# A cross-attention and RWKV kernel on one core: probabilities turned by a second set of score products in place of transposes

## The chip, the cores and the metric

One core of one Trainium2 chip runs the whole program. The metric is device time in microseconds (us) from launch to end; the kernel was run three times, and the median counts. The profile is one further execution, seen by the hardware profiler. Engines are named as in the profile: PE multiplies matrices (PEld is its weight load), DVE, ACT and POOL work on vectors, SP issues transfers. SBUF is the memory on the core, PSUM the eight banks that PE writes, DRAM the memory beside the core.

## The reference, cut to what matters

Sixteen sequences of T = 112 tokens, width D = 512, attend with 16 heads of 32 to 375 context rows each; an RWKV block (token mixing, a recurrence along the tokens with decays, a gated feed-forward) follows. Everything is float32. The change lies in the attention:

```python
a = _layer_norm(audio_kv, ln_gamma, ln_beta)
Q = (hidden_states @ Wq.T).reshape(B, Tt, HEADS, HEAD_DIM).transpose(0, 2, 1, 3)
K = (a @ Wk.T).reshape(B, Ta, HEADS, HEAD_DIM).transpose(0, 2, 1, 3)
V = (a @ Wv.T).reshape(B, Ta, HEADS, HEAD_DIM).transpose(0, 2, 1, 3)
scores = jnp.einsum('bhtd,bhsd->bhts', Q, K) * scale
scores = jnp.where(mask, scores, jnp.float32(-jnp.inf))
attn = jax.nn.softmax(scores, axis=-1)
out = jnp.einsum('bhts,bhsd->bhtd', attn, V)
out = out.transpose(0, 2, 1, 3).reshape(B, Tt, D) @ Wo.T
return hidden_states + jnp.tanh(gate) * out
```

## The kernel before, in words

**Layout.** Activations lie with features on partitions: `x` is (128, 4 chunks, tokens), and a group g of two sequences (224 tokens) is worked at a time; there are eight groups. Four heads of 32 fill one chunk of 128 features, so a step of the attention is a pair (b, m): sequence b, chunk m, four heads. There are 64 steps.

**One step of the attention.** `scores` (L289) makes four products, one a head, with the query as weights (32 x 112) and the keys moving (375 columns). The four use the four row groups of PE, 32 rows each, and four PSUM banks of pool `ps_s`, which has four. The query is scaled by minus one over the root of 32, so the scores are negated and the softmax's maximum is a minimum here. L312 on DVE adds the mask, writes `pr` (112 tokens on partitions, 375 keys) and the row minimum `mn`. `exponentials` (L318) turns `pr` into exp(mn - pr) on ACT, with the row sums in `dens`. In the next step `transposed` (L328) transposes `pr` on PE in three thirds of 125 keys, four heads into one bank of `ps_s` for each third; L339 (ACT) or L341 (DVE) copies the bank to `prT` (125 keys on partitions, 4 x 112). For the first four sequences DVE copies two of three, after that one. In the step after that `outputs` (L344) multiplies by the values: 12 products, keys contracted, weights 125 x 32, into one bank of `ps_mm`, which has two; L356 copies it to `oR`. After four steps `divide` (L358) applies the sums.

**What runs beside it.** `context_units` makes keys (L237, copied by L243 to `kT`) and values (L248, L253) for the next sequence, `query_units` and `project_units` the projections through `project` (L175, matmuls on L181), whose weights come as slabs of 512 KB through SP (L154). The RWKV block has four parts for each group: `front`, `begin`, `middle`, `back`. `front` uses all four banks of `ps_s` three times a group (pxm, L588 and L603), and DVE takes them out in `mixed` (L565). `middle` is the recurrence, 16 steps n a group: `spread` (L744) loads the value rows of a step in four transfers kv<-vd from DRAM (L752, SP), two steps ahead; POOL and DVE multiply by the keys (L765); DVE scans (L788) with decays in PSUM and products in SBUF; POOL multiplies by the receptances (L792); PE sums (L804).

**What sets the order.** All parts are Python generators. A loop at the end of the kernel (L961) always advances the part whose place on a common scale is lowest; the amounts that a part yields are its costs, so the yields set how the parts interleave. The framework then orders each engine's instructions statically, by priority and readiness; `tc.high_priority(AHEAD)` puts an instruction 400 places ahead. It also sets all semaphores and gives out the buffers (`bufs` for each tag). `planned_after` adds an order without a wait. Every engine queue, SP's too, works in order: an instruction that waits holds those behind it.

Of the kernel before, what the change touches and what calls it, by code (L numbers as in the profile page):

```python
# [7 lines left out]
F32 = mybir.dt.float32  # L8
# [5 lines left out]
P = 128  # L14
# [35 lines left out]
def xattn_rwkv_kernel(ctx: ExitStack, tc: tile.TileContext, ins: dict, out: bass.AP):  # L50
# [39 lines left out]
    eps = keep.tile([P, 1], F32, name="eps")  # L90
    tgate = keep.tile([P, 1], F32, name="tgate")
    minus_half = keep.tile([P, NSC], F32, name="minus_half")
    wk = keep.tile([P, NC, D], F32, name="wk")
    wv = keep.tile([P, NC, D], F32, name="wv")
    maa1 = keep.tile([P, NC, NF * DM], F32, name="maa1")
# [14 lines left out]
    def load_mask(b, after=None):  # L110
        mrows[b] = sm.tile([T, S], U8, tag="mrow", name=f"mrow_{b}", bufs=2)
        load = nc.sync.dma_start(
            mrows[b], ins["mask_row"][b * S : (b + 1) * S].partition_broadcast(T)
        )
        if after is not None:
            planned_after(load, after)
# [97 lines left out]
    def context_units(b):  # L214

        raw = raws.pop(b)
        aT = ctxp.tile([P, NC, S], F32, tag="aT", name=f"aT_{b}")

        def turn(k):
            pt = mm_tile(f"pa_{b}_{k}")  # L220
            for c in range(NSC):
                nc.tensor.transpose(
                    pt[:, c * SC : (c + 1) * SC], raw[:, c, k * P : (k + 1) * P],
                    ident[:SC, :SC],
                )
            with tc.high_priority(AHEAD):
                nc.scalar.activation(
                    aT[:, k, :], pt[:, :S], AF.Identity, bias=vec(R_B0, k), scale=vec(R_G0, k)
                )

        kTs[b] = kT = []
        vs[b] = v = kvp.tile([SC, NSC, D], F32, tag="v", name=f"v_{b}")

        def key(m):
            pk = mm_tile(f"pk_{b}_{m}")
            for k in range(NC):
                nc.tensor.matmul(  # L237
                    pk[:, :S], wk[:, k, m * P : (m + 1) * P], aT[:, k, :],
                    start=(k == 0), stop=(k == NC - 1),
                )  # L240
            kT.append(kvp.tile([P, S], F32, tag="kT", name=f"kT_{b}_{m}", bufs=6))
            with tc.high_priority(AHEAD):
                nc.scalar.copy(kT[m], pk[:, :S])  # L243

        def value(c):
            pv = mm_tile(f"pv_{b}_{c}")
            for k in range(NC):
                nc.tensor.matmul(  # L248
                    pv[:SC, :], aT[:, k, c * SC : (c + 1) * SC], wv[:, k, :],
                    start=(k == 0), stop=(k == NC - 1),  # L250
                )
            with tc.high_priority(AHEAD):
                nc.scalar.copy(v[:, c, :], pv[:SC, :])  # L253

        return (
            [(0.5, lambda k=k: turn(k)) for k in range(NC)]
            + [(2.6, lambda m=m: key(m)) for m in range(NC)]
            + [(3.5, lambda c=c: value(c)) for c in range(NSC)]
        )
# [29 lines left out]
    def scores(b, m):  # L289

        if m == 0:
            masks[b] = mb = hp.tile([T, S], F32, tag="mb", name=f"mb_{b}", bufs=1)
            nc.gpsimd.tensor_scalar(mb, mrows.pop(b), -BIG, BIG, ALU.mult, ALU.add)  # L293
            mns[b] = sm.tile([T, H0], F32, tag="mn", name=f"mn_{b}")
            dens[b] = sm.tile([T, H0], F32, tag="den", name=f"den_{b}")
        qT, kT, mb, t0 = qTs[b // GB], kTs[b][m], masks[b], (b % GB) * T
        pss = []
        for hh in range(4):
            r = HD * hh
            ps = ps_s.tile([P, 512], F32, tag="s", name=f"ps_{b}_{m}_{hh}")  # L300
            score = nc.tensor.matmul(  # L301
                ps[:T, :S], qT[r : r + HD, m, t0 : t0 + T], kT[r : r + HD, :],
                start=True, stop=True,
            )
            pss.append(ps)
        prs = []
        for hh in range(4):
            h = 4 * m + hh
            mn = mns[b][:, h : h + 1]
            pr = hp.tile([T, S], F32, tag="pr", name=f"pr_{b}_{h}", bufs=8)  # L310
            with tc.high_priority(AHEAD):
                nc.vector.tensor_tensor_reduce(  # L312
                    pr, pss[hh][:T, :S], mb, 1.0, 3.0e38, ALU.add, ALU.min, mn
                )
            prs.append(pr)
        return prs, score

    def exponentials(b, m, prs, after):  # L318
        for hh, pr in enumerate(prs):
# [5 lines left out]
            if after is not None:  # L325
                planned_after(exp, after)

    def transposed(b, m, c, prs):  # L328

        pt = ps_s.tile([P, 512], F32, tag="s", name=f"pt_{b}_{m}_{c}")  # L330
        for hh in range(4):
            nc.tensor.transpose(  # L332
                pt[:SC, hh * T : (hh + 1) * T], prs[hh][:, c * SC : (c + 1) * SC], ident[:T, :T]
            )
        prT = hp.tile([SC, 4, T], F32, tag="prT", name=f"prT_{b}_{m}_{c}")

        with tc.high_priority(AHEAD):
            if (c == 1) == (b < 4):
                nc.scalar.copy(prT, pt[:SC, : 4 * T])  # L339
            else:  # L340
                nc.vector.tensor_copy(prT, pt[:SC, : 4 * T])  # L341
        return prT

    def outputs(b, m, prTs, oR):  # L344

        po = ps_mm.tile([P, 512], F32, tag="mm", name=f"po_{b}_{m}")
        v = vs[b]
        for c in range(NSC):
            for hh in range(4):
                lo = (4 * m + hh) * HD  # L350
                nc.tensor.matmul(
                    po[hh * HD : (hh + 1) * HD, :T], v[:, c, lo : lo + HD], prTs[c][:, hh, :],
                    start=(c == 0), stop=(c == NSC - 1),
                )
        with tc.high_priority(AHEAD):
            return nc.scalar.copy(oR[:, m, :], po[:, :T])  # L356
# [26 lines left out]
    def attention():  # L383
# [9 lines left out]
        for i in range(NC * B + 2):  # L393
            b, m = divmod(i, NC)
            if i < NC * B:
                if m == 0:
                    g = b // GB
                    if b % GB == 0 and g + 1 < NG:
                        xg[g + 1] = load_x(g + 1)
                    if b + 1 < B:  # L400
                        units += context_units(b + 1)
                        if (b + 1) % GB == 0:
                            units += query_units(g + 1)
                prs, score = scores(b, m)
                if m == 2 and b + 2 < B:
                    load_ahead(b + 2, score)
                if m == 3 and b + 2 < B:
                    normalise(b + 2, score)
                yield 0.9
            copied = None  # L410
            if ready:
                bb, bm, prTs = ready
                if bm == 0:
                    oR = kvp.tile([P, NC, T], F32, tag="oR", name=f"oR_{bb}", bufs=1)
                copied = outputs(bb, bm, prTs, oR)
            if i < NC * B:
                exponentials(b, m, prs, copied)
            if ready:
                yield 0.8
            todo = -(-len(units) // (NC - m)) if i < NC * B else len(units)  # L420
            mine, units = units[:todo], units[todo:]
            mine = mine + [(0.0, lambda: None)] * (3 - len(mine))
            if ready and bm == NC - 1:
                mine[0][1]()
                yield mine[0][0]
                mine[0] = (0.0, lambda: None)
                divide(bb, oR)
                yield 0.6
                if bb % GB == GB - 1:
                    mine = mine[1:2] + project_units(bb // GB) + mine[2:]  # L430
            ready = None
            if before:
                bb, bm, bprs = before
                prTs = []
                for c in range(NSC):
                    if c != 1:
                        mine[c // 2][1]()
                        yield mine[c // 2][0]
                    prTs.append(transposed(bb, bm, c, bprs))
                    yield 0.5  # L440
                ready = bb, bm, prTs
                mine = mine[2:]
            for cost, unit in mine:
                unit()
                yield cost
            before = (b, m, prs) if i < NC * B else None
        for cost, unit in units:
            unit()
            yield cost
# [492 lines left out]
    next(att)  # L942
    nc.sync.dma_start(wv, ins["wv"])
    load_mask(0)
    nc.sync.dma_start(consts, ins["consts"])
    nc.sync.dma_start(st01, ins["st01"])
    nc.sync.dma_start(maa1, ins["maa1"])
# [49 lines left out]
def _layout(inp):  # L997
# [6 lines left out]
    def chunks(m):  # L1004
# [14 lines left out]
        "x": chunks(a["x"].reshape(B * T, D).T),  # L1019
        "ctx": ctx,  # L1020
        "mask_row": mask.reshape(-1),
        "st01": ctx[:, 0:2].reshape(B, 2, NC, P).transpose(3, 1, 2, 0),

        "s0": ctx[:, 2 : 2 + NS].reshape(NG, GB, NC, P, NS).transpose(3, 0, 2, 4, 1),
# [41 lines left out]
```

## Time and profile before

| what | value |
|---|---|
| runs | 1441.12, 1436.12 and 1443.88 us; median 1441.12 us |
| profiled execution | span 1432.1 us from first to last instruction; no other time is given for it |
| median of the runs less that span | 9.0 us |
| busy PE, DVE, POOL, ACT | 1338.5, 904.1, 658.5, 658.4 us |
| chain that ended last | PE 60%, DVE 13%, DMA 9%, POOL 6%, ACT 5%, issue 5%, SP's queue 2% |
| first and last score product | 41.5 and 1190.8 us |
| transposes L332 | 768 instructions, 47.9 to 1205.9 us |
| transfers on SP's queue | 169.7 MB, 38.7% of 16 DMA engines |

A line of the groups gives line, engine, operation, output<-inputs by name, shapes and the count; after the bar stand busy us, mean ns of one, and then the idle time of the engine just before them with what ended it. A line of the timeline gives start, length, engine and line, and how many instructions of the same kind are merged in it. A line of the waits gives who waited for whom, us in total, how often, and the longest. PE's ends are modelled and overlap; starts are measured. A float32 matmul call shows as two instructions, a transpose as one.

### The profile page before, as it was taken

How to read it: one execution, taken by the hardware profiler on the slowest of the kernel's cores; microseconds unless marked ns; L12 is line 12 of the kernel's file. 1: busy time of each engine (PE TensorE's matmuls, PEld its weight loads, DVE VectorE, ACT ScalarE, POOL GpSimd, SP SyncE). 2: the span in 40 equal slices, each digit the busy share in tenths (PEclk: the TensorE clock that was granted, in tenths of full speed). 3: DMA queues.
4: the chain of work that ended last, by engine and by line, in shares of the span. 5: the costliest groups of instructions: out<-in, count | busy, mean ns of one | idle time of the engine just before them, and what ended most of it. 6: DMA issues, size and time to landing. Idle time of an engine off the chain costs nothing.

```text
span 1432.1 us, 23383 instructions
## 1 busy us (share of the span) xinstructions
PE 1338.5 (93%) x8516; PEld 952.2 (66%) x8516; DVE 904.1 (63%) x1750; ACT 658.4 (46%) x1528; POOL 658.5 (46%) x643
## 2 busy tenths in 40 slices
PE   8999998999999999999999999999999998878777
PEld 5557585757676677757676576856777576657556
DVE  2334647883777665874677747775658648875842
ACT  2444532664435653564435644455434446423332
POOL 3001236733555346542556335553466426765840
PEclk9999999999999999999999999999999999979878
DMA  8012035403644055522655036441554034436531
GB/s 264 28 53 82 2 117 160 151 31 103 181 131 158 30 152 176 155 76 76 179 164 167 16 109 186 135 143 30 161 175 154 32 105 148 150 96 184 169 116 55
DMA packets 114666, 171.80 MB, mean 120 GB/s; under 512 B 9768, under 2 KB 87464, under 8 KB 114296
## 3 DMA queue, kind: packets, MB, share of 16 engines
q1 hardware_dynamic: 113912, 169.69, 38.7%
q8 instruction: 67, 1.10, 0.3%
q10 hardware_dynamic: 576, 0.52, 0.1%
q14 instruction: 47, 0.39, 0.1%
q0 software_dynamic: 64, 0.10, 0.0%
HBM read 162.95 MB, written 7.34 MB: 119 GB/s over the span
## 4 chain that ended last, share of the span: by engine, by line
PE 60%; DVE 13%; DMA 9%; POOL 6%; ACT 5%; issue 5%; SPq 2%; ACTq 0%; DVEq 0%; POOLq 0%
PE pv L248 9%; PE pk L237 6%; DMA kv<-vd 4%; PE ps L301 4%; PE pt L332 4%; PE pfk L181 4%; PE pfv L181 3%; PE po L181 3%; PE acc L804 3%; DVE st L788 3%; PE pq L181 3%; SPq L752 2%; PE pv L181 2%; DVE xm L565 2%; PE pfr L181 2%
## 5 line engine op out<-in xcount | busy, mean ns | idle before, releaser
L792 POOL TENSOR_TENSOR st<-st,r 128x448 f32<-128x448 f32 x256 | 320.3, 1263 | 192.7 <-DVE st L788 191.7
L788 DVE TENSOR_TENSOR_SCAN st<-wp,kv 128x448 f32<-128x448 f32 x256 | 269.2, 1077 | 121.9 <-ACT qT L268 31.0
L765 POOL TENSOR_TENSOR kv<-kv,k 128x444 f32<-128x444 f32 x128 | 151.6, 1186 | 92.5 <-DMA kv<-vd 89.1
L237 PE MATMUL pk<-aT,wk 128*128 128x375 f32 x512 | 176.5, 487 | 1.4 <-ACT kT L243 1.2
L248 PE MATMUL pv<-wv,aT 128*125 128x512 f32 x384 | 176.0, 601 | 0.5
L321 ACT ACTIVATE pr<-pr,mn 112x375 f32<-112x375 f32 x256 | 152.9, 600 | 22.4 <-DVE mn L312 22.4
L312 DVE CUSTOM_DVE_ANT_0 pr<-ps,mb 112x375 f32<-112x375 f32 x256 | 127.1, 542 | 51.3 <-PE ps L301 50.6
L237 PEld LDWEIGHTS pk<-aT,wk 128*128 128x128 f32 x512 | 94.8, 192 | 55.8 <-issue 4.0
L332 PEld LDWEIGHTS pt<-ident,pr 112*125 112x125 f32 x768 | 104.0, 192 | 33.6 <-issue 13.9
L248 PEld LDWEIGHTS pv<-wv,aT 128*125 128x125 f32 x384 | 68.4, 187 | 80.6 <-issue 76.6
L332 PE MATMUL pt<-ident,pr 112*125 112x112 f32 x768 | 112.9, 279 | 5.9 <-DVE xm L565 5.9
L765 DVE TENSOR_TENSOR kv<-kv,k 128x444 f32<-128x444 f32 x128 | 101.5, 793 | 1.4 <-DMA kv<-vd 1.4
L804 PE MATMUL acc<-st,consts 128*32 128x224 f32 x1024 | 80.7, 378 | 11.6 <-POOL st L792 9.8
L301 PE MATMUL ps<-kT,qT 32*112 32x375 f32 x512 | 84.6, 521 | 0.2 <-DVE xm L565 0.2
L470 ACT ACT_TABLE_LOAD x64 | 82.1, 1283 | 1.1
L571 POOL TENSOR_TENSOR xm<-xm,xa 128x448 f32<-128x448 f32 x48 | 59.4, 1255 | 35.1 <-DVE xm L565 35.1
L339 ACT COPY prT<-pt 125x448 f32<-125x448 f32 x112 | 59.1, 528 | 33.8 <-PE pt L332 33.5
L181 PE MATMUL pq<-x,wq 128*128 128x224 f32 x256 | 55.5, 371 | 13.1 <-DVE own L731 7.7
L293 POOL TENSOR_SCALAR mb<-mrow 112x375 f32<-112x375 uint8 x16 | 9.0, 560 | 126.0 <-DVE mn L312 123.1
L341 DVE COPY prT<-pt 125x448 f32<-125x448 f32 x80 | 48.7, 608 | 25.9 <-PE pt L332 25.9
L565 DVE SCALAR_TENSOR_TENSOR xm<-pxm,vecs,sx 128x224 f32<-128x224 f32 x128 | 47.3, 442 | 28.0 <-PE pxm L588 28.0
L181 PE MATMUL pfk<-xk,wfk 128*128 128x224 f32 x256 | 55.9, 372 | 7.1 <-DVE xk L900 4.0
(147 smaller groups left out, 2329.1 us busy)
## 6 DMA issues: line engine op xcount, KB each, us to landing
kv<-vd SPq DMA_DIRECT2D x512, 111.5 KB
wo<-in_wo SPq DMA_DIRECT2D x32, 512.0 KB
ctx<-in_ctx SPq DMA_DIRECT2D x15, 750.0 KB
wv<-in_wv SPq DMA_DIRECT2D x16, 512.0 KB
wk<-in_wk SPq DMA_DIRECT2D x16, 512.0 KB
wr<-in_wr SPq DMA_DIRECT2D x16, 512.0 KB
wg<-in_wg SPq DMA_DIRECT2D x16, 512.0 KB
wfk<-in_wfk SPq DMA_DIRECT2D x16, 512.0 KB
```

Source lines behind the costliest of these rows:

```text
L181: mm_ = nc.tensor.matmul(ps[:, e * N : (e + 1) * N], w[:, k, e * P : (e + 1) * P], rhs[:, k, :], start=(k == 0), stop=(k == NC - 1),)
L237: nc.tensor.matmul(pk[:, :S], wk[:, k, m * P : (m + 1) * P], aT[:, k, :], start=(k == 0), stop=(k == NC - 1),)
L248: nc.tensor.matmul(pv[:SC, :], aT[:, k, c * SC : (c + 1) * SC], wv[:, k, :], start=(k == 0), stop=(k == NC - 1),)
L301: score = nc.tensor.matmul(ps[:T, :S], qT[r : r + HD, m, t0 : t0 + T], kT[r : r + HD, :], start=True, stop=True,)
L312: nc.vector.tensor_tensor_reduce(pr, pss[hh][:T, :S], mb, 1.0, 3.0e38, ALU.add, ALU.min, mn)
L321: exp = nc.scalar.activation(pr, pr, AF.Exp, bias=mns[b][:, h : h + 1], scale=-1.0, accum_out=dens[b][:, h : h + 1],)
L332: nc.tensor.transpose(pt[:SC, hh * T : (hh + 1) * T], prs[hh][:, c * SC : (c + 1) * SC], ident[:T, :T])
L470: nc.scalar.preload_act_table_set(table)
L765: product = engine.tensor_tensor(kv4[:, two(p), :, 1:T], kv4[:, two(p), :, 1:T], k_prev.unsqueeze(1).broadcast_to([P, 2, GB, T - 1]), ALU. ...
L788: scan = nc.vector.tensor_tensor_scan(flat(pair), w_ps[c], flat(kv[:, two(p), :]), 0.0, ALU.mult, ALU.add)
L792: nc.gpsimd.tensor_tensor(pair, pair, rs[c // 2][:, c % 2, :].unsqueeze(1).broadcast_to([P, 2, N]), ALU.mult,)
L804: part = nc.tensor.matmul(accs[c][32 * q : 32 * q + 32, :], consts[:, C_WIN + 32 * e : C_WIN + 32 * e + 32], st[:, q, :], start=(e == 0), ...
```

## The change

`transposed` goes. `turned` makes the scores a second time with the keys as weights (32 x 125) and the query moving (112 columns), so that keys lie on partitions: 12 products a step, four heads side by side in four row groups, the four banks of `ps_s` at once, the three thirds next to each other in a head's bank. The softmax needs the row minimum of each token for every key. It is one number a token and head, on the token's partition, and is now wanted along the free axis on all 125 key partitions: `scores` stores four columns of `mn` to DRAM (`low`, 112 x 4) and loads them back to 125 partitions (`lows`), both through SP. DVE subtracts `lows` from the scores in PSUM (four instructions a step, 3 x 112 elements, `lows` read with a step of four words and repeated for the three thirds), and ACT makes the exponentials (three a step, 4 x 112) with the mask as a bias that belongs to the key's partition (`key_bias`). The first exponentials stay, for the row sums. `turned` stands where the first two transposed thirds stood, after the step's first unit; the other units follow it. Buffers: `kT` 6 to 7, `pr` 8 to 4, `prT` three of 448 elements to one of 1344.

```diff
+    key_masks = keep.tile([SC, B * NSC], U8, name="key_masks")
+    key_bias = keep.tile([SC, B * NSC], F32, name="key_bias")
...
-            kT.append(kvp.tile([P, S], F32, tag="kT", name=f"kT_{b}_{m}", bufs=6))
+            kT.append(kvp.tile([P, S], F32, tag="kT", name=f"kT_{b}_{m}", bufs=7))
...
-            pr = hp.tile([T, S], F32, tag="pr", name=f"pr_{b}_{h}", bufs=8)
+            pr = hp.tile([T, S], F32, tag="pr", name=f"pr_{b}_{h}", bufs=4)
...
-        return prs, score
+        low = dram.tile([T, 4], F32, tag="low", name=f"low_{b}_{m}")
+        lows = hp.tile([SC, T, 4], F32, tag="lows", name=f"lows_{b}_{m}", bufs=2)
+        with tc.high_priority(AHEAD):
+            nc.sync.dma_start(low, mns[b][:, 4 * m : 4 * m + 4])
+            nc.sync.dma_start(lows, low.partition_broadcast(SC))
+        return prs, lows, score
...
-    def transposed(b, m, c, prs):
...
+    def turned(b, m, lows):
+
+        qT, kT, t0 = qTs[b // GB], kTs[b][m], (b % GB) * T
+        pts = [
+            ps_s.tile([P, 512], F32, tag="s", name=f"pt_{b}_{m}_{hh}") for hh in range(4)
+        ]
+        for c in range(NSC):
+            for hh in range(4):
+                r = HD * hh
+                nc.tensor.matmul(
+                    pts[hh][:SC, c * T : (c + 1) * T], kT[r : r + HD, c * SC : (c + 1) * SC],
+                    qT[r : r + HD, m, t0 : t0 + T], start=True, stop=True,
+                )
+        prT = hp.tile([SC, 4, NSC, T], F32, tag="prT", name=f"prT_{b}_{m}", bufs=1)
         with tc.high_priority(AHEAD):
-            if (c == 1) == (b < 4):
-                nc.scalar.copy(prT, pt[:SC, : 4 * T])
-            else:
-                nc.vector.tensor_copy(prT, pt[:SC, : 4 * T])
+            for hh in range(4):
+                nc.vector.tensor_tensor(
+                    prT[:, hh], pts[hh][:SC, : NSC * T].rearrange("p (c t) -> p c t", c=NSC),
+                    lows[:, :, hh].unsqueeze(1).broadcast_to([SC, NSC, T]), ALU.subtract,
+                )
+            for c in range(NSC):
+                nc.scalar.activation(
+                    prT[:, :, c, :], prT[:, :, c, :], AF.Exp,
+                    bias=key_bias[:, b * NSC + c : b * NSC + c + 1], scale=-1.0,
+                )
         return prT
...
-                prTs = []
-                for c in range(NSC):
-                    if c != 1:
-                        mine[c // 2][1]()
-                        yield mine[c // 2][0]
-                    prTs.append(transposed(bb, bm, c, bprs))
-                    yield 0.5
-                ready = bb, bm, prTs
-                mine = mine[2:]
+                mine[0][1]()
+                yield mine[0][0]
+                ready = *before[:2], turned(*before)
+                mine = mine[1:]
+                yield 1.5
...
+    nc.sync.dma_start(key_masks, ins["mask_cols"])
+    nc.gpsimd.tensor_scalar(key_bias, key_masks, BIG, -BIG, ALU.mult, ALU.add)
```

`outputs` reads `prT[:, hh, c, :]` in place of `prTs[c][:, hh, :]`, and the inputs get `mask_cols`, the mask with keys on partitions.

More of the change, by code (lines that the diff above doesn't have):

```diff
@@ L326, in exponentials, with outputs @@
                 planned_after(exp, after)
-    def transposed(b, m, c, prs):
[L330 to L335, printed above, removed]
-        with tc.high_priority(AHEAD):
-            if (c == 1) == (b < 4):
-                nc.scalar.copy(prT, pt[:SC, : 4 * T])
-            else:
-                nc.vector.tensor_copy(prT, pt[:SC, : 4 * T])
+    def turned(b, m, lows):
[11 more added lines that the diff above has]
+        prT = hp.tile([SC, 4, NSC, T], F32, tag="prT", name=f"prT_{b}_{m}", bufs=1)
+        with tc.high_priority(AHEAD):
+            for hh in range(4):
[8 more added lines that the diff above has]
+                )
         return prT
-    def outputs(b, m, prTs, oR):
+    def outputs(b, m, prT, oR):
         po = ps_mm.tile([P, 512], F32, tag="mm", name=f"po_{b}_{m}")
@@ L351, in outputs @@
                 nc.tensor.matmul(
-                    po[hh * HD : (hh + 1) * HD, :T], v[:, c, lo : lo + HD], prTs[c][:, hh, :],
+                    po[hh * HD : (hh + 1) * HD, :T], v[:, c, lo : lo + HD], prT[:, hh, c, :],
                     start=(c == 0), stop=(c == NSC - 1),
@@ L403, in attention @@
                             units += query_units(g + 1)
-                prs, score = scores(b, m)
+                prs, lows, score = scores(b, m)
                 if m == 2 and b + 2 < B:
@@ L411, in attention @@
             if ready:
-                bb, bm, prTs = ready
+                bb, bm, prT = ready
                 if bm == 0:
                     oR = kvp.tile([P, NC, T], F32, tag="oR", name=f"oR_{bb}", bufs=1)
-                copied = outputs(bb, bm, prTs, oR)
+                copied = outputs(bb, bm, prT, oR)
             if i < NC * B:
@@ L432, in attention @@
             if before:
-                bb, bm, bprs = before
-                prTs = []
-                for c in range(NSC):
-                    if c != 1:
-                        mine[c // 2][1]()
-                        yield mine[c // 2][0]
-                    prTs.append(transposed(bb, bm, c, bprs))
-                    yield 0.5
-                ready = bb, bm, prTs
-                mine = mine[2:]
+                mine[0][1]()
[3 more added lines that the diff above has]
+                yield 1.5
             for cost, unit in mine:
@@ L445, in attention @@
                 yield cost
-            before = (b, m, prs) if i < NC * B else None
+            before = (b, m, lows) if i < NC * B else None
         for cost, unit in units:
@@ L1021, in _layout @@
         "mask_row": mask.reshape(-1),
+        "mask_cols": mask.reshape(B, NSC, SC).transpose(2, 0, 1).reshape(SC, B * NSC),
         "st01": ctx[:, 0:2].reshape(B, 2, NC, P).transpose(3, 1, 2, 0),
```

## The prediction

> **What bounds the kernel now.** I read the busy shares first, then a table of stretches of the span, then the groups by line, then single stretches of the PE timeline, then the waits. Busy shares of the page:
>
> ```profile
> span 1432.1 us, 23383 instructions
> PE 1338.5 (93%) x8516; PEld 952.2 (66%) x8516; DVE 904.1 (63%) x1750; ACT 658.4 (46%) x1528; POOL 658.5 (46%) x643
> ```
>
> The table of stretches (length, then busy time of PE, PEld, DVE, ACT, POOL, then PE clock, DMA share, GB/s) says where that share is made:
>
> ```profile
> 200.00:1100.00 900.00, 869.62 (x5736) 621.52 (x5735) 611.09 (x1180) 442.10 (x1043) 456.14 (x433) 1.00 0.42 127
> 1210.00:1432.10 222.10, 177.20 (x936) 137.08 (x934) 140.48 (x199) 79.54 (x146) 117.87 (x98) 0.86 0.42 131
> ```
>
> While attention runs beside the recurrence (200 to 1100 us), PE is busy 96.6%, DVE 68%, ACT 49%. After 1210 us no attention is left, so the change can't touch that stretch except by shifting it. So a microsecond of PE work saved before 1210 us is a microsecond of the end, if no other engine makes PE wait for it. The groups that the change removes or multiplies (columns: busy us, mean ns of one, idle before them and its releaser):
>
> ```profile
> L332 PE MATMUL pt<-ident,pr 112*125 112x112 f32 x768 | 112.9, 279 | 5.9 <-DVE xm L565 5.9
> L339 ACT COPY prT<-pt 125x448 f32<-125x448 f32 x112 | 59.1, 528 | 33.8 <-PE pt L332 33.5
> L341 DVE COPY prT<-pt 125x448 f32<-125x448 f32 x80 | 48.7, 608 | 25.9 <-PE pt L332 25.9
> L788 DVE TENSOR_TENSOR_SCAN st<-wp,kv 128x448 f32<-128x448 f32 x256 | 269.2, 1077 | 121.9 <-ACT qT L268 31.0
> ```
>
> The busy time of PE counts modelled, overlapping ends, so I price PE work from start to start in its timeline (start, length, line, count):
>
> ```profile
> 71.90 1.02 PE L332 MATMUL pt<-ident,pr 112*125 112x112 f32 x8
> 72.77 3.61 PE L248 MATMUL pv<-wv,aT 128*125 128x512 f32 x8
> ...
> 304.51 1.04 PE L588 MATMUL pxm<-th,maa 32*128 32x224 f32 x16
> 305.48 1.02 PE L642 MATMUL gv<-gsq,consts 128*128 128x448 f32 x2
> ...
> 707.41 0.59 PE L332 MATMUL pt<-ident,pr 112*125 112x112 f32 x4
> 707.93 1.02 PE L718 MATMUL pw<-thd,td 64*128 64x224 f32 x4
> ...
> 716.57 0.90 PE L301 MATMUL ps<-kT,qT 32*112 32x375 f32 x8
> 717.40 0.78 PE L351 MATMUL po<-prT,v 125*32 125x112 f32 x24
> 718.11 3.70 PE L248 MATMUL pv<-wv,aT 128*125 128x512 f32 x8
> ```
>
> **PE: a gain.** Twelve transposes of one step (b, m) hold PE 0.52 us (four) plus 0.87 us (eight), 1.39 us; 64 steps make 89 us. In their place stand twelve matmuls a step. Each call is two instructions (256 score calls show as 512), so 24, of 112 columns, on 32 rows, four row groups side by side: six rounds of four. Three rows bound them. The outputs, also 24 instructions of 112 columns in four groups, take 0.71 us (717.40 to 718.11), but load weights only 32 wide: the floor. The pxm products, 32 rows and weights 128 wide, need 0.97 us for four rounds of twice the columns; six rounds at that pace would be 1.46 us: the ceiling, where weight loads set the pace. The scores, 0.83 us for two rounds of 375 columns, give 0.42 a round against 0.24 for 224: a line through both falls to 0.12 us at 112 columns, 0.69 in all. I take 0.80, near the floor. Saved: 0.59 x 64 = **-38 us** (ends -44 and +4).
>
> [...]
>
> **DVE: the main cost.** 80 copies (48.7 us) go; 256 subtractions of 336 elements come, with scores from PSUM and `lows` from SBUF. The nearest operation is the product of L378 (PSUM by SBUF, 448 elements, 613 ns); with L812 (224 elements, 382 ns) a line gives 498 ns for 336. But `lows[:, :, hh]` takes one word of every four, and no DVE row of this trace reads at a step over more than 8 elements; rows of neighbours are a floor. The slowest DVE row by element with the same two memories is the scan, 1077/448 = 2.40 ns, which gives 808 ns. I take 0.81, because the step is what sets the new read apart and the floor has no room for it. Added: 207 - 49 = 158 us, 2.5 us a step (at 0.50: 80 us, 1.24 a step). 44 of the 64 steps start between 200 and 1100 us: DVE goes from 0.68 to 0.80 there (0.74 at 0.50). DVE is an in-order queue that frees PSUM banks for PE, and the new four stand ahead of scans, `mixed` and score minima. PE's rows of waiting for DVE add up to 34 us now. If waiting grows as share/(1 - share), 2.1 to 4.0, it nearly doubles: **+30 us** (+12 at 0.50). The banks are in this term: a transposed third took one score bank and gave it back after one copy; `turned` needs all four at its first round and gives the last back after four subtractions. Scores to the first transposes are mostly 4 us and more apart, but around the pxm products, which use the same four banks three times in some 20 us, only 0.3 to 0.9 us are left.
>
> [...]
>
> **ACT.** 112 copies (59.1 us) go, 192 exponentials of 448 come; the row of L475 (448 elements, 580 ns) makes 111 us. ACT goes from 49 to about 53% in the stretch; the cover is its idle half. PE's waits for ACT add up to 27 us now; the same rule gives **+5** (ends 0 and +10). `exponentials` stays whole, since the sums come from it.
>
> **SP and the transfers.** A step adds two issues on SP: `low` waits for the four minima, `lows` for `low` to land. Behind them in SP's order stand the quartets kv<-vd of the scans, weight slabs, the next context. The waits:
>
> ```profile
> SPq L752 <- DMA vd<-v: 24.4, 8, 3.8
> ```
> ```profile
> POOL kv L765 <- DMA kv<-vd: 89.1, 33, 24.2
> ```
>
> The first is SP waiting for a DRAM store to land, 3 us each; in the critical chain those stores take 4.0 to 4.2 us, for 224 KB where `low` has 1.8 KB. With the issues (0.36 and 0.58 us by vd and kv) SP is held some 4 us a step. The second says that POOL already waits for kv, so this cover is thin. PE's waits for POOL are 17 us, 0.19 of those 89. If every second hold delays a quartet by 2 us, POOL waits 64 us more and PE **+12** (ends 0 and, with each hold at 4 us, +49). `lows` itself: minima done 4.1 us after the scores start (716.57 to 720.69), 0.4 + 4.1 for `low`, 0.6 + 5 for `lows` (kv, half its bytes, lands in 3.3 to 5.0; end 10): 14 us. From scores to the transposes of the same step are mostly 15 us and more, but 7.2 at 118.7, 10.6 at 76.7, 11.6 at 1163.7 us: about 13 us late there, of which I count **+7** (ends 0 and, if SP runs behind everywhere, +60).
>
> The mask columns and `key_bias` are two instructions in the load-bound start; the buffers that change in number are free before they are needed (`pr` after its exponential, a step earlier than the next minima): 0, with ends -2 and +5.
>
> **Sum.** -38 + 30 + 5 + 12 + 7 = +16 us on the span of 1432.1. The page gives the profiled execution no time beside its span; the median of the runs, 1441.1, lies 9.0 above it, which I leave as it is: **1457 us**.
>
> **The rivals.**
> *PE's saving arrives, faster.* For it: PE is 97% busy, DVE has a third of its time left, `lows` has a whole step to travel. It decides if a subtraction takes 0.50 to 0.55 us: then -38 + 12 + 0 to 5, 1415 to 1430, say 1420. Against it: the kv cover that is already gone in places.
> *Even.* A subtraction of some 0.65 us: DVE at 0.77, +20 in place of +30, with SP at half: -38 + 20 + 5 + 6 + 7 = 0, 1441.
> *`lows` late everywhere.* SP reaches `low` behind a slab or kv wait; DVE stands at the subtraction with scans behind it: +60 in place of +7, about 1510.
> *The matmuls are no cheaper than the transposes* (1.46 us a step): PE +4 in place of -38, 1499.
>
> **Chances.** Slower as forecast 0.42 (own range 1447 to 1490), faster 0.36, even 0.11, late 0.06, no cheaper 0.05. The range 1412 to 1500 reaches over the first three and up to the fifth; outside stay the late case and the ends of the others. By sign, with 0.5% (7 us, about what a measurement of this kernel can tell from no change): faster 0.36, same 0.11, slower 0.53.
>
> **What would show it.** In the changed profile: 24 matmuls of the turned scores in 0.7 to 0.9 us start to start (the PE step; 1.4 would be the last rival); the subtraction's mean, 500 or 800 ns (it decides the sign); DVE near 0.80 between 200 and 1100 us, with PE waiting for DVE rows for about 60 us; SP waits for `low` near 3 us each and POOL's wait for kv above 89 us; DVE waits for `lows` rare. I am wrong if the subtraction is at its floor, or if PE's stretch is as full as before with less work in it.

## The result and the profile after

Before 1440.6 us (1436.1 to 1443.9), after **1563.6 us** (1551.4 to 1573.1): ratio 1.084, interval [1.080, 1.089]. The change makes the kernel 123 us slower where +16 was forecast. The profiled execution of after has a span of 1549.6 us, 117.5 more than that of before.

The busy shares and the chain that ended last, from the page of after:

```profile
span 1549.6 us, 25491 instructions
PE 1403.7 (91%) x9284; PEld 959.1 (62%) x9284; DVE 1032.1 (67%) x1926; ACT 714.8 (46%) x1607; POOL 656.8 (42%) x644
...
PE 49%; DVE 20%; DMA 11%; ACT 7%; issue 5%; POOL 5%; SPq 2%; ACTq 0%; DVEq 0%; POOLq 0%
```

PE's share of the chain falls from 60 to 49%, DVE's rises from 13 to 20%. PE has 1549.6 - 1403.7 = 146 us without work, before 94: 52 us of the 117. The granted clock is 0.937, before 0.970; busy time times the missing share of the clock grows from 40 to 88 us, an estimate of what PE loses by running slower. Whether the slower clock is a cause of the loss or follows from the waits, no run here separates. The same stretch as before, and the stretch from the last sequence's mask to the end (before 292.1 us long):

```profile
200.00:1100.00 900.00, 834.93 (x5779) 572.67 (x5778) 642.16 (x1194) 445.96 (x1005) 407.89 (x390) 0.97 0.44 126
1229.00:1549.60 320.60, 264.48 (x1511) 197.88 (x1509) 195.58 (x310) 118.79 (x243) 149.33 (x130) 0.84 0.40 121
```

DVE's share in the first is 71%, not the 80% foreseen, and for a bad reason: everything goes on more slowly, DVE's other work too. The groups that the change brought, and above them the product that waits for kv:

```profile
L778 POOL TENSOR_TENSOR kv<-kv,k 128x444 f32<-128x444 f32 x128 | 152.4, 1193 | 212.6 <-DMA kv<-vd 187.5
L351 DVE TENSOR_TENSOR prT<-pt,lows 125x336 f32<-125x336 f32 x256 | 176.3, 747 | 25.8 <-PE pt L344 7.4
...
L356 ACT ACTIVATE prT<-prT,key_bias 125x448 f32<-125x448 f32 x192 | 114.9, 658 | 151.7 <-DVE prT L351 151.5
```

The subtraction takes 747 ns (four in a row 2.75 us, 0.69 each), near the 0.81 us taken. The turned scores, in PE's timeline:

```profile
756.61 0.80 PE L239 MATMUL pk<-aT,wk 128*128 128x375 f32 x2
757.33 0.92 PE L344 MATMUL pt<-qT,kT 32*125 32x112 f32 x24
758.18 3.29 PE L183 MATMUL pr<-xm,wr 128*128 128x224 f32 x16
```

An undisturbed step holds PE 758.18 - 757.33 = 0.85 us, near the 0.80 taken. So both prices were right, and the sum was wrong. The waits of SP's queue:

```profile
SPq L321 <- DVE mn L314: 502.8, 53, 23.6
SPq L765 <- DVE st L801: 120.8, 44, 10.8
SPq L322 <- DMA low<-mn: 93.8, 56, 6.7
```

SP stands 503 us at `low` for the minima and 94 at `lows` for `low`: 9.3 us a step, not 4. The value rows kv<-vd are queued behind, and POOL's wait for them grows from 89.1 to 187.5 us. One case, first SP's timeline, then pieces of the critical chain of the same stretch:

```profile
749.38 0.48 SPq L133 DMA_DIRECT2D ctx<-in_ctx  x1
753.85 0.34 SPq L321 DMA_DIRECT2D low<-mn  x1
...
761.92 0.26 SPq L322 DMA_DIRECT2D lows<-low  x1
762.27 2.47 SPq L765 DMA_DIRECT2D kv<-vd  x4
```
```profile
753.85 8.05 DMA low<-mn
761.92 0.26 SPq L322
...
764.17 5.43 DMA kv<-vd
769.70 0.20 ACT kv L788
```

`low` is 1.8 KB, but it lands 8.05 us after its issue, behind a context of 750 KB that was issued 4.5 us earlier. The kv quartet is issued at 762.27, when SP comes free, lands at 769.6, and ACT and then PE's decays (pw) follow. That is the chain.

This landing is the longest of 64. From the issue of `low` to that of `lows` SP takes under 1.5 us in 30 steps and 2.6 us on average; 12 steps take 4.7 to 8.1 us. Each of these 12 has a context or a weight slab issued 0.5 to 5.3 us ahead of `low`, and none of the other 52 has one in the 8 us ahead.

### The profile page after: what moved, and what is told of

The parts are those of the page before. It is cut to its first block, busy times and chain, and to the rows that moved or that the text cites. A ratio compares the mean times of both kernels' runs of the same rounds, so it can differ in the third digit from the quotient of the medians.

```text
span 1549.6 us, 25491 instructions
## 1 busy us (share of the span) xinstructions
PE 1403.7 (91%) x9284; PEld 959.1 (62%) x9284; DVE 1032.1 (67%) x1926; ACT 714.8 (46%) x1607; POOL 656.8 (42%) x644
## 2 busy tenths in 40 slices
DMA packets 131319, 186.40 MB, mean 120 GB/s; under 512 B 18410, under 2 KB 104106, under 8 KB 130938
## 4 chain that ended last, share of the span: by engine, by line
PE 49%; DVE 20%; DMA 11%; ACT 7%; issue 5%; POOL 5%; SPq 2%; ACTq 0%; DVEq 0%; POOLq 0%
PE pv L250 7%; DMA kv<-vd 6%; PE pk L239 5%; DVE st L801 4%; DVE prT L351 3%; POOL st L805 3%; PE pt L344 3%; PE pfv L183 3%; PE ps L303 3%; PE pq L183 3%; DMA low<-mn 2%; DVE xm L578 2%; PE pp L183 2%; PE pfr L183 2%; PE pfk L183 2%
## 5 line engine op out<-in xcount | busy, mean ns | idle before, releaser
L778 POOL TENSOR_TENSOR kv<-kv,k 128x444 f32<-128x444 f32 x128 | 152.4, 1193 | 212.6 <-DMA kv<-vd 187.5
L351 DVE TENSOR_TENSOR prT<-pt,lows 125x336 f32<-125x336 f32 x256 | 176.3, 747 | 25.8 <-PE pt L344 7.4
L239 PE MATMUL pk<-aT,wk 128*128 128x375 f32 x512 | 181.4, 498 | 9.5 <-ACT oR L374 6.1
L356 ACT ACTIVATE prT<-prT,key_bias 125x448 f32<-125x448 f32 x192 | 114.9, 658 | 151.7 <-DVE prT L351 151.5
L778 DVE TENSOR_TENSOR kv<-kv,k 128x444 f32<-128x444 f32 x128 | 109.2, 853 | 32.7 <-DMA kv<-vd 32.5
L344 PEld LDWEIGHTS pt<-qT,kT 32*125 32x125 f32 x1536 | 73.0, 194 | 47.5 <-issue 16.0
L817 PE MATMUL acc<-st,consts 128*32 128x224 f32 x1024 | 86.2, 378 | 17.6 <-POOL st L805 16.1
L344 PE MATMUL pt<-qT,kT 32*125 32x112 f32 x1536 | 91.9, 301 | 10.2 <-DVE mn L314 3.7
L303 PE MATMUL ps<-kT,qT 32*112 32x375 f32 x512 | 90.3, 535 | 5.6 <-ACT qT L270 3.4
L183 PE MATMUL pp<-qT,wo 128*128 128x224 f32 x256 | 59.9, 394 | 7.8 <-ACT kT L245 4.5
L817 PEld LDWEIGHTS acc<-st,consts 128*32 128x32 f32 x1024 | 23.8, 110 | 66.3 <-issue 30.3
```

What stands on the lines that cost most here:

```text
L183: mm_ = nc.tensor.matmul(ps[:, e * N : (e + 1) * N], w[:, k, e * P : (e + 1) * P], rhs[:, k, :], start=(k == 0), stop=(k == NC - 1),)
L239: nc.tensor.matmul(pk[:, :S], wk[:, k, m * P : (m + 1) * P], aT[:, k, :], start=(k == 0), stop=(k == NC - 1),)
L303: score = nc.tensor.matmul(ps[:T, :S], qT[r : r + HD, m, t0 : t0 + T], kT[r : r + HD, :], start=True, stop=True,)
L344: nc.tensor.matmul(pts[hh][:SC, c * T : (c + 1) * T], kT[r : r + HD, c * SC : (c + 1) * SC], qT[r : r + HD, m, t0 : t0 + T], start=True, s ...
L351: nc.vector.tensor_tensor(prT[:, hh], pts[hh][:SC, : NSC * T].rearrange("p (c t) -> p c t", c=NSC), lows[:, :, hh].unsqueeze(1).broadcast_ ...
L356: nc.scalar.activation(prT[:, :, c, :], prT[:, :, c, :], AF.Exp, bias=key_bias[:, b * NSC + c : b * NSC + c + 1], scale=-1.0,)
```

## The experiments

Times are medians; the ratio goes against the kernel before on the same chip (1437.7 to 1440.0). Line numbers shift by some lines between kernels.

| kernel | us | ratio, interval |
|---|---|---|
| b_together | 1434.4 | 0.998 [0.995, 1.002] |
| b_together_act | 1442.0 | 1.001 [0.997, 1.004] |
| b_early_transfers | 1451.8 | 1.009 [1.005, 1.013] |
| b_one_wait | 1462.0 | 1.017 [1.012, 1.022] |
| b_transfers | 1478.3 | 1.029 [1.022, 1.036] |
| a_exp_from_psum | 1451.5 | 1.010 [1.005, 1.016] |
| a_exp_prT2 | 1453.7 | 1.011 [1.007, 1.014] |
| a_exp_pr6 | 1454.4 | 1.011 [1.007, 1.014] |
| a_copies | 1465.1 | 1.018 [1.012, 1.024] |
| a_pairs | 1471.0 | 1.022 [1.016, 1.028] |
| a_exp_dve_load | 1493.4 | 1.039 [1.032, 1.045] |
| a_no_transfers_unit | 1493.6 | 1.039 [1.031, 1.047] |
| a_no_transfers | 1523.9 | 1.059 [1.052, 1.067] |
| a_permuted | 1531.4 | 1.065 [1.058, 1.072] |
| b_free_transfers | 1539.0 | 1.069 [1.062, 1.076] |
| a_queue_gpsimd | 1588.5 | 1.105 [1.097, 1.112] |
| a_unit_step | 1724.0 | 1.197 [1.191, 1.203] |

### The transfers alone, taken away and added

Taken from after (the constant has the shape and the step of `lows`):

```diff
-            nc.sync.dma_start(low, mns[b][:, 4 * m : 4 * m + 4])
-            nc.sync.dma_start(lows, low.partition_broadcast(SC))
-        return prs, lows, score
+        return prs, fixed_lows, score
```

> The changed kernel without low and lows: the subtraction reads a constant tile of the same shape and step, so the row minima are left out of the second exponentials. PE and DVE keep their order. If the transfers (SP held behind the minima and behind the store, so kv late) are the main cost, the time falls by 60 us or more, to 1500 or below, and POOL's wait for kv falls from 188 us to about 90. If DVE's subtractions and the four banks are the main cost, it falls by less than 25 us and POOL's wait for kv stays near 190.

Added to before, with nothing that reads them (`lows` goes to DRAM, so nothing waits for it):

> The kernel before with the two transfers of each step added and their result used by nobody (lows is spread to a DRAM tile, since SBUF has no room; transposes and copies stay). PE and DVE keep their order. If the transfers are the main cost, it is slower by 60 us or more, about 1500 to 1520, with POOL waiting for kv near 190 us. If they cost only together with the subtraction, it stays within 15 us of 1441.

Both answer alike: 1563.6 to 1523.9 is 40 us off (and POOL's wait for kv falls to 73 us), 1437.7 to 1478.3 is 41 us on. Both lie between the ranges of the two theories: the transfers are a third of the loss. Then the transfers on before without one wait, and without both:

```diff
-            nc.sync.dma_start(low, mns[b][:, 4 * m : 4 * m + 4])
-            nc.sync.dma_start(lows, low.partition_broadcast(SC))
+            planned_after(nc.sync.dma_start(low, kT[:T, :4]), score)
+            planned_after(nc.sync.dma_start(lows, fixed_low.partition_broadcast(SC)), score)
```

> As the kernel before with the two transfers a step (1478), but lows reads a constant, goes ahead of low on SP and does not wait for it to land; low still waits for the minima. If the hold is the landing (94 us of SP's waits): 1445 to 1458. If it is the wait for the minima (418 us of SP's waits) or the traffic: 1468 to 1482; the run in which neither waits tells those two apart.

> The kernel before with the two transfers a step in the same places of SP's order, but low reads a corner of the step's keys (made earlier) in place of the minima, and lows reads a constant, so that SP waits for neither the minima nor low to land; nothing reads them. The run with both waits was 1478 against 1438. Theory 'the hold of SP's order': 1438 to 1450, and POOL's wait for kv near the 89 us of before. Rival 'the traffic (219 KB a step) and the issues': 1465 to 1485, POOL's wait for kv 130 us and more.

The waits of b_transfers, b_one_wait and b_early_transfers, in this order:

```profile
SPq L319 <- DVE mn L312: 417.9, 51, 22.5
SPq L320 <- DMA low<-mn: 93.8, 60, 4.5
...
POOL kv L770 <- DMA kv<-vd: 167.1, 54, 9.5
```
```profile
SPq L323 <- DVE mn L316: 451.0, 51, 25.8
...
POOL kv L774 <- DMA kv<-vd: 139.8, 44, 23.6
```
```profile
POOL kv L774 <- DMA kv<-vd: 127.7, 36, 23.9
```

With neither wait +12 us, with the wait for the minima +22, with both +40. Neither theory holds alone: about 12 us are the traffic and the issues, 10 the wait for the minima, 18 the wait for `low` to land. Each time has an interval of 5 to 10 us either way, too wide to rank these parts. But the length of a row is not its price: 418 us of waiting for minima cost some 10, 94 us of waiting for the landing some 18. A likely reason, not shown, is that in much of the first wait SP has nothing urgent behind it.

An earlier kernel for the same question did not answer it:

> The kernel before with the same two transfers a step, of the same shape and in the same place on SP, but read from constants, so that neither waits for a minimum nor for the other; nothing reads them. The earlier run with the waits was 1478 us against 1438. Theory 'SP is held in order, and what stands behind (weights, kv, context) starts late': without the waits 1440 to 1450, POOL's wait for kv back near 90 us. Rival 'the traffic and the issues themselves cost it': 1465 to 1485 again, POOL's wait for kv near 167 us.

It took 1539 us. With nothing to wait for, the static order put most of the 64 loads at the front of SP's queue, ahead of most contexts: PE is busy 113 of the first 200 us (before 188), and DVE waits 120 us for contexts. It says nothing on the hold, and the two kernels above, which tie the transfers to their step, replace it.

Another queue (both issues on `nc.gpsimd`, nothing else changed):

> The kernel after with both transfers issued on POOL's queue in place of SP's. Hold theory: SP is free as in the kernel before, but POOL now stands at the minima and at low, 4 to 10 us a step, with its products kv behind; POOL is busy 42%, so part of this is covered: 1530 to 1560, with POOL's wait for the DMA of kv under 120 us and a new wait of POOL for DVE and low. Rival 'traffic': the same as after, 1555 to 1575. A third way: POOL's own hold delays the products more than SP's did, 1580 and more.

The waits of a_queue_gpsimd:

```profile
POOL low L321 <- DVE mn L314: 197.3, 45, 13.0
...
POOL lows L322 <- DMA low<-mn: 79.3, 39, 7.9
...
POOL kv L778 <- DMA kv<-vd: 53.1, 25, 14.9
```

1588 us, the third way. SP is free again and kv comes early (53 us of waiting, less than before), but POOL stands 277 us at the two issues, and its products and receptances are queued behind. Here the hold moved with the instruction.

### The step of four words

The constant of a_no_transfers laid out as neighbours (`[SC, 4, T]` in place of `[SC, T, 4]`):

> The kernel after without the transfers, the minima replaced by a constant, as in the earlier run of 1524 us, but the constant is laid out as neighbours. It prices the step by itself, free of transfers. Step theory: subtraction 500 to 560 ns instead of 749, time 1480 to 1505. Rival (the pass itself): subtraction 749 ns, time 1518 to 1530.

The group of the subtraction, first a_no_transfers, then a_no_transfers_unit:

```profile
L348 DVE TENSOR_TENSOR prT<-pt,fixed_lows 125x336 f32<-125x336 f32 x256 | 176.6, 749 | 21.6 <-PE pt L341 7.9
```
```profile
L348 DVE TENSOR_TENSOR prT<-pt,fixed_lows 125x336 f32<-125x336 f32 x256 | 111.8, 495 | 21.2 <-PE pt L341 7.4
```

495 ns is what the line through the rows of neighbours gave (498). The step of four words costs 254 ns an instruction (0.76 ns an element), 65 us of DVE, 30 us of time.

Two ways to give the whole kernel neighbours. In the first the store turns the order, word by word:

> The kernel after, with the minima stored head by head, so that each subtraction reads 112 neighbouring words and not one word of every four; transfers stay. Theory 'the step is what makes the subtraction dear' (the prediction's 0.81 us against 0.50 us for neighbours): the mean of the subtraction falls from 747 ns to 500 to 560 ns, DVE loses 48 to 63 us, and the time falls by 20 to 40 us, to 1525 to 1545. Rival 'the price is that of the pass itself, PSUM by SBUF, 3 x 112': the mean stays within 5% of 747 ns and the time within 1% of 1564. The store is now of single words, so the lows may also land a little later, up to +10 us.

1724 us, far outside the 1525 to 1545 expected. The subtraction falls to 496 ns, but the packets under 512 bytes rise from 18410 to 39914, SP's wait for `low` to land from 94 to 447 us, and POOL's for kv from 187.5 to 379. SP's waits:

```profile
SPq L322 <- DMA low<-mn: 446.7, 60, 12.0
SPq L321 <- DVE mn L314: 312.9, 46, 16.8
```

In the second POOL copies `lows` into the other order (`lows` has one buffer there, not two):

```diff
+            near = hp.tile([SC, 4, T], F32, tag="near", name=f"near_{b}_{m}", bufs=1)
+            nc.gpsimd.tensor_copy(near, lows.rearrange("p t h -> p h t"))
-        return prs, lows, score
+        return prs, near, score
```

> The kernel after, whole, with one more operation: POOL copies each lows into the order in which the subtraction reads neighbours (one copy of 448 a step), so the transfers stay as they are. The step cost 30 us where there were no transfers (1524 to 1494). Expected from that: 1563 less 30, and up to 15 back for POOL's 64 copies (about 75 us of its idle half): 1530 to 1550, with the subtraction at 500 ns. If POOL's copy makes kv late instead: 1555 and more.

1531 us: the 30 us come back, for 70 us of POOL's idle time. It is the best whole form of the change that I ran, and 91 us slower than before.

### The pass on DVE: its load or its place

From after, without transfers and subtraction (ACT reads PSUM):

```diff
-                nc.vector.tensor_tensor(
-                    prT[:, hh], pts[hh][:SC, : NSC * T].rearrange("p (c t) -> p c t", c=NSC),
-                    lows[:, :, hh].unsqueeze(1).broadcast_to([SC, NSC, T]), ALU.subtract,
-                )
...
+                nc.scalar.activation(
+                    prT[:, hh], pts[hh][:SC, : NSC * T].rearrange("p (c t) -> p c t", c=NSC),
+                    AF.Exp, bias=fixed, scale=-1.0,
+                )
```

> The changed kernel with neither transfers nor subtraction: ACT makes the second exponentials straight from PSUM, one of 336 elements for each head, with a constant bias; row minima and mask of these exponentials are left out. This leaves the score products in place of the transposes. If PE's saving of some 33 us (0.86 for 1.39 us a step) is real and nothing else stands in the way, it takes 1405 to 1425. If the four banks at once stall PE whoever empties them, it stays above 1441.

1451.5 us, above before and in the range of the second theory; the next section takes this up. Against a_no_transfers_unit the pass costs 42 us with neighbours, against a_no_transfers 72. Then the same kernel with four subtractions a step that nothing waits for:

> The kernel after with the exponentials straight from PSUM on ACT (1451 us; no subtraction, minima, mask or transfers there), and beside them, on DVE, four subtractions of 336 neighbours a step from SBUF constants into a tile that nothing reads. It gives DVE's load without the wait: neither ACT nor PSUM's banks wait for these. The run with the subtraction on the path, also on neighbours (495 ns), was 1494. Theory 'DVE's share makes PE wait': 1475 to 1495. Theory 'the pass stands between PE's banks and ACT, so its place is what costs': 1450 to 1462.

1493.4 us, the same as with the subtraction on the path, though no bank and no exponential waits for these. So DVE's load alone can cost time. But the load came out larger than meant: 173 us, 677 ns each, where the pass has 112; POOL's busy time rises by 11 us too. By DVE time, 42/173 = 0.24 us are lost per us of idle load, and 42/112 = 72/192 = 0.375 per us of the pass (192 = 256 x 749 ns). An estimate from these: two thirds of the price is the load, a third the place. In PE's time the 42 us are 20 us more without work (its waits for DVE go from 28 to 42 us, those for ACT from 35 to 40) and 22 us more busy; the granted clock falls from 0.965 to 0.953, which by busy time makes some 17 of these, an estimate.

### The scores a second time

> The kernel before with its twelve transposes of a step in one place, after the first unit, as turned stands in the changed kernel; nothing else. If the new place and the order that the planner makes of it cost by themselves, it is slower by 20 us or more (above 1460). If not, it stays within 10 us of 1441.

> The kernel before with the twelve transposes in one place (1434 in an earlier run), and all 192 copies out of PSUM on ACT (112 before), so ACT has 42 us more and DVE 49 us less to do. Theory 'ACT is what the exponentials from PSUM cost': 1443 to 1455. Rival 'ACT's free half covers it': 1425 to 1440.

Neither run can be told from no change: the place (1434) costs nothing that shows, and the copies moved from DVE to ACT (1442, between the two ranges) nothing either. That DVE has 49 us less to do there may hide a price of ACT's load. Then the turned scores with copies as in before:

```diff
+                src = pts[hh][:SC, : NSC * T].rearrange("p (c t) -> p c t", c=NSC)
+                if (hh == 1) == (b < 4):
+                    nc.scalar.copy(prT[:, hh], src)
+                else:
+                    nc.vector.tensor_copy(prT[:, hh], src)
```

> The change's PE part by itself: the kernel after with the turned scores, but what leaves PSUM is copied as in the kernel before (four copies of 336 a step, 160 on ACT and 96 on DVE, where before had 112 and 80 of 448); no second exponential, no subtraction, no transfers, so the scores stand where the probabilities should. Theory 'PE's saving is real and the load on ACT eats it' (24 matmuls hold PE 0.85 us where twelve transposes in one place hold 1.30, 29 us in all; the run with exponentials straight from PSUM was still 1451): 1405 to 1418. Rival 'the four banks at once, and PE's stalls and clock, eat it': 1430 to 1450.

1465 us, above both ranges: PE's part alone, without any of the costs that I had counted against it, is 25 us slower than before, with DVE and ACT about as busy (907.7 and 667.9 against 904.1 and 658.4 us). The same eight sequences (from the mask of the sixth to that of the fourteenth) in before and in a_copies:

```profile
299.00:965.00 666.00, 644.43 (x4248) 462.40 (x4244) 444.00 (x866) 331.83 (x773) 327.59 (x312) 1.00 0.41 126
```
```profile
308.00:978.00 670.00, 647.92 (x4619) 452.17 (x4608) 445.29 (x861) 338.32 (x804) 331.74 (x312) 0.99 0.41 126
```

PE is as full as before, though 32 steps of cheaper work are in it. Adding up PE's timeline there (from each start to its end or the next start): the transposes hold PE 48.6 us in before (1.52 a step) and 45.4 in b_together (1.42), the turned scores 41.2 in a_copies (1.29). Not 0.85, for two reasons. A step that PE's static order breaks costs more: rounds of four are cut, three calls take 0.41 us and the other nine 0.83. 20 of 64 steps are broken, as in b_together (19), so that isn't the work of the four banks; transposes lose little when broken (5 and 7 take 0.64 and 0.76 for 1.30 whole). And behind the pxm products, which hold the same four banks, a step takes 1.9 to 2.4 us. An unbroken step elsewhere keeps to 0.85 to 0.92. The second reason is the larger: of eight steps of a group two stand behind pxm and take 2.6 us more than two whole ones, two others are broken and take 0.8 more. In b_together the two behind pxm take 0.4 us more than whole ones.

Do two heads at a time help?

> The kernel after with the exponentials straight from PSUM (1451), the turned scores made two heads at a time, so that the first six matmul calls need two free banks and not four; only two row groups run side by side. In the run of copies and in after, PE leaves the 24 matmuls after one, two or three calls or stands in them behind the pxm products, so that 32 steps hold PE 41 us where 32 x 0.85 is 27. Theory 'four banks at once is what eats PE's saving': fewer breaks, and the total at or under 1451 (1440 to 1452) although a step alone is longer. Rival 'four row groups side by side matter more': 1455 to 1480.

1471 us, 20 more than with four. The whole step now takes 1.16 us:

```profile
61.41 1.23 PE L341 MATMUL pt<-qT,kT 32*125 32x112 f32 x24
62.56 0.90 PE L241 MATMUL pk<-aT,wk 128*128 128x375 f32 x2
```

Added up as above, the 64 steps hold PE 95.6 us, in a_exp_from_psum 81.8: 14 of the 20 us. So four row groups side by side do matter. But the run relieves nothing at the banks: 21 steps are broken (20 there), and behind pxm a step still takes 1.9 to 2.7 us. The theory of the four banks gains no support, and what they cost stays unmeasured. Last, the buffers that the change took (the first gives `prT` two and `kT` six again, the second `pr` six):

> The kernel after with the exponentials straight from PSUM (1451 us), but with two buffers of turned probabilities and not one (kT back to 6 for the room); every engine's order stays as it is. Theory 'the single large prT makes ACT, and behind it PE, wait for the outputs': 1425 to 1442. Rival 'the buffers are free in time, as predicted': 1446 to 1457.

> The same, but six buffers of masked scores pr in place of four (before had eight); prT as in the kernel after. Theory 'the minima wait for the exponentials of the step before, because pr has four buffers': 1425 to 1442. Rival 'free in time': 1446 to 1457.

1453.7 and 1454.4: buffers cost nothing that shows, as the prediction had it. **Open** stays why the turned scores without subtraction end 14 us above before (25 with copies), when their own slots give back about 15 of PE's time. The place and the buffers are excluded as its main cause, and so, by a_copies, is more work on ACT or DVE; the four banks are not. The profiled a_exp_from_psum, 17 us longer than before, loses 18 us up to the mask of the sixth sequence (316.6 us against 299.1) and 8 in the next eight sequences, and wins 8 back after the last mask. In its first 200 us the granted clock is 0.93 against 0.98 in before, in 180 to 200 us 0.63 against 1.00. What sets it off was not isolated.

## Why the prediction was wrong, by its own steps

The runs form a ladder from before to after, so each term has its measured size. The steps don't add up exactly, since each set of runs has its own before. The copies that go (49 us of DVE) lie in the first row, while the prediction's DVE term has them.

| step | predicted | measured | from |
|---|---|---|---|
| scores a second time, exponentials on ACT | -38 + 5 = -33 | +14 | before to a_exp_from_psum |
| subtraction, neighbours | +12 (its 0.50 case) | +42 | to a_no_transfers_unit |
| its step of four words | +18 (30 less 12) | +30 | to a_no_transfers |
| transfers, `lows` late | +12 + 7 | +40 | to after |
| sum | +16 | +126 | |

- **PE, -38.** The new slot was right (0.80, measured 0.85), the old one nearly (1.39, in one place 1.30). The failure is that one undisturbed slot was multiplied by 64: over the steps as they stand the saving is 0.23 a step, 15 us, and even this doesn't reach the end. In place of -33 the runs show +14, or +25 in a_copies.
- **DVE, +30.** The price of the subtraction was right, its effect about twice what I took: 72 us for the whole 192 us of it, and by the same rate some 59 (an estimate) for the 158 us that the +30 stood for. I let the load act only through PE's waits for DVE (34 to 64 us foreseen); they grew to 40. Part of the loss surfaces a step further: ACT waits 151.5 us for the subtraction, and PE's waits for ACT go from 27 to 70 us (46 without the transfers). Part, by the estimate for a_exp_dve_load, where no engine waits for the load, is PE at a lower granted clock (0.965 to 0.953, some 17 of 42 us). A load on an in-order engine could not be priced here from the rows of the bottleneck's direct waits.
- **ACT, +5.** Its load wasn't priced by itself: in b_together_act DVE has less to do at the same time. PE's waits for ACT grow with the subtraction and the transfers (35 us in a_exp_from_psum, 46 in a_no_transfers, 70 in after).
- **SP, +12.** SP is held 9.3 us a step, not 4: I left out the minima's wait (7.9), while the landing, priced at 3 us, is 1.5 us of waiting a step. That kv is late and POOL waits was right: 89 to 187.5 us, foreseen 153. The path from there to PE was wrong. I took 0.19 of POOL's wait, through PE's waits for POOL; in b_transfers these grow only from 17 to 24 us. Those for ACT, which I had left out of this path, grow from 27 to 49, most of it in one row (before, then b_transfers):

```profile
PE gv L642 <- ACT gsq L639: 3.6, 2, 2.3
```
```profile
PE gv L647 <- ACT gsq L644: 19.4, 8, 4.3
```

- **`lows` late, +7, and the rival "late everywhere".** Wrong: DVE waited for `lows` once, 1.9 us. In b_transfers, where nothing reads them, they cost 41 us as well, and POOL's wait for kv goes from 89.1 to 167.1 us: they cost mostly by what stands behind them, not by arriving late.
- **The clock** was in no term. In after the granted clock falls even where PE hardly stands: in 130 to 140 us it is 0.66 with PE busy 9.73 of 10 us, in before 1.00 (after, then before). The products for the keys in that stretch take 842 ns each, in before 478. Why the clock falls is not shown.

```profile
130.00:140.00 10.00, 9.73 (x59) 5.03 (x61) 2.57 (x10) 5.14 (x14) 0.00 (x0) 0.66 0.44 122
```
```profile
130.00:140.00 10.00, 9.80 (x52) 7.71 (x50) 2.52 (x4) 0.77 (x2) 1.79 (x2) 1.00 0.46 147
```

The rival "the matmuls are no cheaper" (+4 in place of -38) came nearest for PE, with the wrong reason: the slot is cheaper, the end isn't.

## What to carry to other kernels

Price an added pass on an in-order engine by the run's own exchange rate, not by one waiting row: here each microsecond of DVE cost 0.24 to 0.375 us though DVE was idle a third of the time. A small transfer that waits on a queue shared with prefetches cost here mostly by what stood behind it (41 us in b_transfers, where nothing reads it); look at what large load was issued just ahead of it (here 12 of 64 steps had one, and SP took 4.7 to 8.1 us in them, 2.6 on average over all), and expect another queue to move the hold, as it did here (277 us on POOL). Multiply a slot by its count only after counting how many slots are whole: here a whole one took 0.85 us, the mean of 32 steps was 1.29.

## What the runs showed of the hardware

Unexpected was the subtraction of two SBUF constants in a_exp_dve_load: 445 to 1899 ns for the same 336 elements. Four take 2.12 us while POOL is idle, as here:

```profile
565.12 2.12 DVE L357 TENSOR_TENSOR waste<-load_a,load_b 125x336 f32<-125x336 f32 x4
```

The four that start at 594.15 us take 4.28 us, beside POOL's copy at 595.00 (0.89 us) and its product at 595.86 (1.12 us); the 2.16 us more are about what these two take. With one input in PSUM the same operation takes 495 ns in the mean and stays at 439 to 510 ns (a_no_transfers_unit). Whether POOL's work is what holds them up, no run here separates.
